# A graph layer on one core: the first product of an edge group in 16-bit passes over 30 nodes a tile, its sums in shifted windows

## The chip, the cores and the metric

The kernel runs on one core of one Trainium2 chip. Its time is the device time of one execution in microseconds (us), given as the median of several runs. A profile is one execution of its own, with its own time. TensorE is called PE in the profile, its weight loads PEld, VectorE DVE, ScalarE ACT, GpSimd POOL, SyncE SP; a small q (SPq) is the engine's queue of instructions and transfers.

## What is computed

One layer of a graph network: 6250 nodes with 128 features, 100000 edges that are sorted by their destination, four attributes an edge.

```python
src = edge_index[0]
dst = edge_index[1]
msg_in = jnp.concatenate([node_features[src], node_features[dst], edge_features], axis=1)
h = jax.nn.silu(msg_in @ mW1 + mb1)
messages = h @ mW2 + mb2
aggregated = jax.ops.segment_sum(messages, dst, num_segments=N)
upd_in = jnp.concatenate([node_features, aggregated], axis=1)
u = jax.nn.silu(upd_in @ uW1 + ub1)
updated = u @ uW2 + ub2
return layer_norm(node_features + updated, ln_g, ln_b)
```

The result of this is added to the input, and one more normalisation over the features follows. With 16 edges a node on average, and destinations in order, 128 edges in a row cover about 8 nodes, and 1024 about 64.

## The kernel before

**Tables.** The first product is taken apart: a node's part as a source, `x @ mW1[:128]`, goes into a table `tab_a` in DRAM, its part as a destination with the bias, `x @ mW1[128:256] + mb1`, into `tab_b`, and the attributes, transposed, into `ea_d`. `tables()` makes all of `tab_a` and the first two batches (of 512 nodes) of `tab_b` before the edges; `make_b` (L457) makes the other 11 batches during the loop.

**Groups.** Edges are worked on in 98 groups of 1024, that is 8 tiles of 128 edges. In 82 of them (`listed`), POOL gathers the rows of `tab_a` by an indirect transfer for each tile (L234), and each further group goes through the following:

- `load` (L578): SP fetches the group's destinations, spread over 80 partitions (`near`, L435), the 80 rows of `tab_b` that start at the group's first node (`mv`, L584), and its 4 rows of attributes, into rows 80 to 83 of `st` (L585).
- `matrices` (L589): DVE makes two one-hot matrices. `st` has a row for each of the 80 nodes and a column for each edge; the same instruction sums its rows into a column of degrees (`deg_at`, L297). `oh` has a row for each edge and 80 columns a tile.
- `before_rows` (L618): for each tile PE multiplies `st` with `mv` into a PSUM tile `pre`; this picks each edge's destination row and adds the attributes' part. All is in 32 bits. `pre` has two buffers (`wide()`, L164).
- `hidden` (L634): DVE adds the gathered rows (L645), ACT applies silu (L646) to give `h`.
- `sums` (L648): for each tile PE multiplies `h` with `oh`, 112 columns of which 80 are used, and adds up the 8 tiles in one PSUM tile `pt`, of which there is one. Every fourth group a transpose puts the columns of degrees into the same tile.
- `add` and `count` (L689, L679): DVE adds `pt` into the sums `acc` of the batch at the group's place, and the degrees into `deg`; the degrees of four groups at once.

**Sorted groups.** The other 16 groups (`by_sort`) are not gathered: their edges are sorted by source at the start, and PE picks the source rows by 16-bit products with one-hot matrices `O` (`po`), from `tab_a` split into three 16-bit parts. Their products stand between those of the listed groups.

**Order.** Each engine's order is written out by hand: the loop over `listed` (L1179) is a row of stages. Stage j of group g asks for the gathers of the group four ahead and the loads three ahead, makes the matrices two ahead, does the first product one ahead, then the work on sorted groups, then the sums of g, and last (`node_stage`, L790) a part of the work on nodes. Half of the gathers are held until PE has reached a certain product (L1244 to L1258); the place is found from the products' work, counted by `matmul(..., share=)` (L147).

**A guard.** `check_1` to `check_4` test that every destination lies within its group's 80 rows. If not, a slow general path (L1360) does all edges again.

Of the kernel before, what the change touches and what calls it, by code (L numbers as in the profile page):

```python
# [10 lines left out]
F32 = mybir.dt.float32  # L11
# [16 lines left out]
def kernel(  # L28
# [28 lines left out]
    W = 80  # L57
    WS = 112
    NW = NP + W
    AW = 768  # L60
    K1 = W + ED
# [146 lines left out]
    w_row_i = first.tile([P, W], I32, name="w_row_i")  # L208
    nc.gpsimd.iota(w_row_i, pattern=[[1, W]], base=0, channel_multiplier=0)
# [13 lines left out]
    tab_b = dram.tile([NW, H], F32, name="tab_b")  # L223
    sd = dram.tile([4, QN * GE], F16, name="sd")
    ea_d = dram.tile([ED, NG * GE], F32, name="ea_d")
# [3 lines left out]
    def fetch(g):  # L229
# [20 lines left out]
        ceil_i, pattern=[[BN * P, NB + 1], [0, G]], base=BN * P - W, channel_multiplier=0  # L250
    )
    pos_i = first.tile([R, P], I32, name="pos_i")
# [9 lines left out]
    if rest:  # L262
        nc.vector.memset(dst_l[low:NG], N)
    nc.sync.dma_start(dst_l[:low], dst[: low * GE].rearrange("(p j) -> p j", j=GE))
# [8 lines left out]
    dst_l = dst_l[:NG]  # L273
    w_row = ps1.tile([P, W], F32, name="w_row")
# [17 lines left out]
    deg_s = []  # L292
    for k in range(3):
        deg_s.append(consts.tile([W, P], F32, name=f"deg_s{k}"))
        nc.vector.memset(deg_s[k], 0.0)

    def deg_at(g):  # L297
        s, i = divmod(g - 1, 4) if g else (-1, 0)
        return deg_s[(s + 1) % 3], 32 * i

    def deg_col(g):
        t, c = deg_at(g)
        return t[:, c : c + 1]
# [19 lines left out]
    def lists_1():  # L323
        base_c = first.tile([NG, 1], F32, name="base_c")
        nc.vector.tensor_copy(base_c, dst_l[:, 0:1])
        rel_n = first.tile([P, GE], F32, name="rel_n")[:NG]
        nc.vector.tensor_scalar(rel_n, dst_l, base_c, None, op0=OP.subtract)
        parts.update(base_c=base_c, rel_n=rel_n)
        nc.vector.memset(floor_i[:, 0:1], 0)
        nc.vector.memset(floor_i[:, last[NB - 2] + 1 :], batches[NB - 1][0] * P)  # L330
        nc.vector.memset(ceil_i[:, 84 + G // 2 :], batches[NB - 1][0] * P - W)
        nc.vector.memset(ceil_i[:, 92 + G // 2 :], NP)
        for g in range(NG):
            k = made_for(g)
            usual = (g + G // 2) // G
            if k < usual and g >= G:
                nc.vector.memset(
                    ceil_i[:, g + G // 2 : g + G // 2 + 1],
                    sum(n for _, n in batches[: k + 1]) * P - W,
                )  # L340

    def lists_2():
# [12 lines left out]
        nc.vector.tensor_copy(base_f, to_row(parts["base_c"], NG))  # L355
        parts["base_f"] = base_f

    def lists_3():
# [3 lines left out]
        nc.vector.tensor_scalar(base_p, p_b[:, :NG], p_col, None, op0=OP.add)  # L362
# [6 lines left out]
        nc.vector.tensor_tensor(base_i, base_f, lim, op=OP.min)  # L369
# [12 lines left out]
    mid = (W - 1) / 2  # L382

    def check_1():
        parts["far"] = first.tile([NG, 2], F32, name="far")
        nc.vector.tensor_reduce(parts["far"][:, 0:1], parts["rel_n"], AX.X, OP.max)

    def check_2():
        far = parts["far"]
        nc.vector.tensor_reduce(far[:, 1:2], parts["rel_n"], AX.X, OP.min)  # L390
# [33 lines left out]
    def attribute_rows(c):  # L424
        t = turn.tile([EQ, ED, EJ], F32, name="ea_t")
        nc.scalar.copy(t, ea_l.pop(c).rearrange("q (j d) -> q d j", d=ED))
        to = ea_d[:, c * EC : (c + 1) * EC]
        nc.scalar.dma_start(to.rearrange("d (q j) -> q d j", q=EQ), t)

    def destinations(g):  # L430
        near[g] = work.tile([P, GE], I32, name="near")[:W]
        n = min(GE, E - g * GE)
        if n < GE:
            nc.vector.memset(near[g][:, n:], N)
        nc.sync.dma_start(  # L435
            near[g][:, :n],
            dst[g * GE : g * GE + n].rearrange("(o e) -> o e", o=1).to_broadcast([W, n]),
        )
# [18 lines left out]
    def make_b(k):  # L457
        i0, n = batches[k]
        pm = bank()
        product(k, 1, pm)  # L460
# [1059 lines left out]
```

## Time and profile before

| | |
|---|---|
| Median of 3 runs | 1079.45 us (1077.62 to 1081.79) |
| Profiled execution, device time | 1078.25 us |
| its span, first to last instruction | 1076.5 us |
| mean granted clock of TensorE | 0.863 |
| instructions | 17905 |
| bytes moved by DMA | 108.94 MB, 101 GB/s |
| gathers, POOL L234 | 654 of about 0.95 us, 0.30 us between two |
| first gather from tab_a | at 68.6 us |
| last gather | issued at 1045.2 us |

The page of a profile gives busy time by engine, then the chain of work that ended last: from the last instruction back to what released it, and so on to the start, with shares of the span. It then lists groups of like instructions, as `line engine op out<-in shapes xcount | busy us, mean ns of one | idle time before them and what ended it`. Most products are recorded on the helper's lines, L148 (`matmul`) and L151 (`transpose`), so they are told apart by what they write: `pre`, `pt`, `po` and `pn`. Matmuls are pipelined, so the mean duration of one is longer than the time from one to the next.

### The profile page before, as it was taken

The page shows a single profiled execution, that of the slowest core. Times are in us where ns is not written, and L with a number is a line of the kernel's source. Part 1 is how long each engine was busy: PE and PEld are TensorE (multiplying, and loading weights), DVE is VectorE, ACT ScalarE, POOL GpSimd, SP SyncE. Part 2 cuts the span into 40 slices and gives each one's busy share as a digit, 9 for nine tenths or more (in the row PEclk, how much of TensorE's full clock was granted, in tenths as well). Part 3 has the DMA queues.
Part 4 walks back from the last instruction along what each step waited for, and adds up shares of the span by engine and source line. Part 5 has one row for each costly group of instructions (what it writes and reads, how often), then busy time and mean ns, then how long its engine had stood idle before and what let it go on. Part 6 is the DMA issues. An engine that isn't in the chain of part 4 may idle for free.

```text
span 1076.5 us, 17905 instructions
## 1 busy us (share of the span) xinstructions
PE 807.8 (75%) x6479; PEld 687.8 (64%) x6479; DVE 558.1 (52%) x1357; ACT 404.1 (38%) x543; POOL 641.9 (60%) x665
## 2 busy tenths in 40 slices
PE   5548557668878788877877878777878877877874
PEld 4548455566757576666776666666577666676653
DVE  3463677843555283555373555444374445473282
ACT  1122114533343354344344353343253344363142
POOL 6646557765656666565666566556566566666550
PEclk8778779789888989798998989879879788999795
DMA  9544315342424252525163443424343434242220
GB/s 231 140 114 117 93 57 143 87 101 81 114 85 116 72 137 76 121 75 131 57 152 84 117 109 97 110 80 100 87 112 93 99 92 120 71 111 81 85 77 25
DMA packets 86890, 108.94 MB, mean 101 GB/s; under 512 B 22348, under 2 KB 63456, under 8 KB 86794
## 3 DMA queue, kind: packets, MB, share of 16 engines
q1 hardware_dynamic: 52498, 58.26, 21.3%
q0 software_dynamic: 20928, 42.90, 15.2%
q10 hardware_dynamic: 13368, 6.56, 2.3%
q8 instruction: 53, 0.87, 0.4%
q14 instruction: 43, 0.35, 0.1%
HBM read 96.26 MB, written 11.40 MB: 100 GB/s over the span
## 4 chain that ended last, share of the span: by engine, by line
PE 52%; issue 16%; DVE 13%; another core or an unknown queue 7%; ACT 5%; DMA 3%; POOL 2%; SPq 1%; DVEq 0%; ACTq 0%; POOLq 0%
PE pt L148 14%; PE po L148 14%; PE pre L148 13%; PE pn L148 8%; PE pn L151 2%; POOL ga L234 2%; DMA ga<-tab_a,src_i 1%; DVE st L593 1%; DVE oh L603 1%; ACT h L646 1%; DVE ga L645 1%; ACT O L1027 1%; PE pre L151 1%; DVE O L1023 1%
## 5 line engine op out<-in xcount | busy, mean ns | idle before, releaser
L234 POOL DMA_INDIRECT ga<-tab_a,src_i x614 | 601.9, 980 | 380.4 <-issue 202.4
L148 PE MATMUL pre<-mv,st 128*128 128x128 f32 x1308 | 202.3, 310 | 27.4 <-issue 12.8
L148 PEld LDWEIGHTS pre<-mv,st 128*128 128x128 f32 x1308 | 190.5, 225 | 40.3 <-issue 29.2
L148 PE MATMUL pt<-oh,h 128*128 128x112 f32 x1308 | 191.5, 305 | 25.6 <-issue 12.6
L148 PEld LDWEIGHTS pt<-oh,h 128*128 128x128 f32 x1308 | 180.1, 218 | 39.5 <-issue 24.3
L646 ACT ACTIVATE h<-ga 128x1024 f32<-128x1024 f32 (+1 forms) x78 | 81.1, 1042 | 317.7 <-DVE ga L645 222.6
L692 DVE TENSOR_TENSOR acc<-acc,pt 128x80 f32 x98 | 23.3, 238 | 341.3 <-PE pt L148 104.1
L148 PE MATMUL po<-O,A_low 128*128 128x157 bf16 (+47 forms) x896 | 163.8, 225 | 22.3 <-issue 22.3
L148 PE MATMUL po<-O,A 128*128 128x156 bf16 (+37 forms) x1376 | 140.2, 227 | 36.6 <-issue 33.0
L148 PEld LDWEIGHTS <-A 128*128 128x128 bf16 x1376 | 112.4, 104 | 58.3 <-issue 57.3
L645 DVE TENSOR_TENSOR ga<-ga,pre 128x1024 f32<-128x1024 f32 (+1 forms) x78 | 93.3, 1197 | 54.7 <-PE po L148 22.0
L593 DVE TENSOR_SCALAR_CACHE_REDUCE st<-near,base_p 80x1024 f32<-80x1024 int32 x82 | 103.4, 1261 | 11.9 <-issue 10.4
L148 PEld LDWEIGHTS <-A_low 128*128 128x128 bf16 x896 | 91.0, 103 | 20.6 <-issue 20.3
L1027 ACT ACTIVATE O<-sc,p_less 128x512 bf16<-128x512 f16 x128 | 84.8, 711 | 1.4 <-DMA sc<-sd 1.4
L1028 ACT ACTIVATE O<-O,ones 128x1024 bf16<-128x1024 bf16 x64 | 73.5, 1148 | 2.1
L603 DVE TENSOR_TENSOR oh<-w_row,rel 128x640 f32<-128x640 f32 x82 | 66.9, 816 | 0.8
L151 PE MATMUL pn<-ident,hT 128*128 128x128 f32 x128 | 23.2, 310 | 45.1 <-issue 10.2
L1070 ACT ACTIVATE hT<-po 128x512 f32<-128x512 f32 x32 | 19.0, 593 | 91.4 <-PE po L148 51.7
L234 POOL DMA_INDIRECT ga<-in_x_dram,src_i x40 | 38.3, 959 | 23.2 <-issue 9.9
L151 PEld LDWEIGHTS pn<-ident,hT 128*128 128x128 f32 x128 | 15.5, 154 | 51.1 <-issue 24.3
L148 PE MATMUL pt<-oh,h_s 128*128 128x112 f32 x256 | 34.8, 290 | 12.6 <-ACT h_s L1079 7.9
L148 PE MATMUL pn<-Oc,at_s 128*128 128x512 f32 x64 | 37.8, 675 | 8.0 <-issue 5.6
(221 smaller groups left out, 921.9 us busy)
## 6 DMA issues: line engine op xcount, KB each, us to landing
near<-in_dst_dram SPq DMA_DIRECT2D x81, 320.0 KB
ga<-tab_a,src_i POOLq DMA_INDIRECT x614
sc<-sd SPq DMA_DIRECT2D x16, 512.0 KB
mv<-tab_b SPq DMA_DIRECT2D x82, 40.0 KB
tab_a<-A SPq DMA_DIRECT2D x11, 256.0 KB
tab_b<-o SPq DMA_DIRECT2D x11, 256.0 KB
out_dram<-o ACTq DMA_DIRECT2D x11, 256.0 KB
x<-in_x_dram SPq DMA_DIRECT2D x10, 256.0 KB
```

The lines of the kernel that those rows point to most:

```text
L148: counted(nc.tensor.matmul(to, *operands, **flags), to, share)
L151: counted(nc.tensor.transpose(to, *operands), to)
L234: ins = nc.gpsimd.indirect_dma_start(out=rows[g][:, i, :], out_offset=None, in_=x if g < RAW else tab_a[:, :], in_offset=bass.IndirectOffs ...
L593: nc.vector.tensor_scalar(stbuf[turn_of(g) % NST][:W], near.pop(g), base_p[:W, g : g + 1], 0.0, op0=OP.is_equal, op1=OP.add, accum_out=deg ...
L603: nc.vector.tensor_tensor(oh[g][:, :n, :W], w_row[:, None, :].to_broadcast([P, n, W]), rel[:, g, :n, None].to_broadcast([P, n, W]), op=OP. ...
L645: nc.vector.tensor_add(s[:, i], s[:, i], p[:, i])
L646: nc.scalar.activation(h[:, i], s[:, i], AF.Silu)
L692: nc.vector.tensor_add(to, to, pt[:, :W])
L1023: nc.vector.tensor_scalar(O[:, j], key, p_rows[:, r : r + 1], None, op0=OP.is_equal)
L1027: nc.scalar.activation(O[:, j], key, AF.Square, bias=p_less[:, r : r + 1])
L1028: nc.scalar.activation(O[:, 2:], O[:, 2:], AF.Relu, bias=ones[:, 0:1], scale=-1.0)
L1070: nc.scalar.activation(now["hT", half], now.pop("po"), AF.Silu)
```

## The change

The group's nodes get a grid: the first node is rounded to a multiple of 8, and tile i looks only at 30 nodes that start 8 i nodes after the group's first.

- **First product.** `st` has 90 rows, 30 nodes in three 16-bit parts each, and 36 rows of attributes (three parts of the attributes times three of their weights); `mv` has 8 blocks of columns, one for each tile. Each tile takes one 16-bit product with 126 rows. The one-hot `st` is made from 16-bit offsets (`off_d`), compared with the row number divided by three.
- **Tables.** `tab_b` stays for the sorted groups; beside it stands `tab_p`, the same in three 16-bit parts, in the order that lets one row of `mv` be 2 KB in a row. A load takes four transfers for `mv`.
- **Sums.** `oh` is filled in 32 of 112 columns, the other 80 stay zero. Tile i adds its 112 columns at column 8 i of `pt`, so `pt` is cleared first by a product of zeros over 256 columns. Degrees come from four products of a column of ones with `oh`, into the same tile. The sums are 88 columns wide.
- **Splitting.** Making a batch of `tab_p`, or a chunk of attributes, is a chain of steps (`begin`, `high`, `middle`, `low`) that are taken at four places in a stage; their PSUM tile is one of the two of `pre`.
- **Weights.** The work of the 16-bit products, of the clearing and of the degrees counts a quarter in the gathers' pacing.

```diff
+    S = 8
+    V, VS, VW = 30, 32, 112
+    WP = S * (G - 1) + VW
+    W = S * (G - 1) + VS
+    D = W // S
+    KB, K1 = 3 * V, 3 * V + 9 * ED
...
+    def b_steps(k, pm):
...
+        def begin():
+            for i in range(BN):
+                matmul(
+                    pm[:m, i, :], xT[k][:, i : n * P : BN], w1[:, 1, :], start=True, stop=True
+                )
+
+        def high():
+            nc.vector.tensor_add(v, v, b1[:m, None, :].to_broadcast([m, BN, H]))
+            nc.scalar.copy(t[:, :, 0], v)
+            tb = node.tile([P, BN, H], F32, name="o")[:m]
+            nc.scalar.copy(tb, v)
...
+        def middle():
+            nc.vector.tensor_sub(v, v, t[:, :, 0])
+            nc.scalar.copy(t[:, :, 1], v)
+
+        def low():
+            nc.vector.tensor_sub(t[:, :, 2], v, t[:, :, 1])
+            d0 = (i0 * P + F) // S
+            for u in range(S // BN):
+                nc.sync.dma_start(
...
-        nc.sync.dma_start(mv[turn_of(g) % NM][:W], tab_b[bass.ds(bases[g], W), :])
-        nc.sync.dma_start(stbuf[turn_of(g) % NST][W:K1], ea_d[:, g * GE : (g + 1) * GE])
+        to = mv[turn_of(g) % NM].rearrange("r i f -> r (i f)")
+        for a in range(D - G + 1):
+            n = min(S, V - a * S)
+            nc.sync.dma_start(
+                to[3 * S * a : 3 * S * a + 3 * n],
+                tab_p[:n, :, bass.ds(bases[g] + a, G), :].rearrange("b s d f -> (b s) (d f)"),
+            )
+        cols = slice(g * GE, (g + 1) * GE)
+        nc.sync.dma_start(
+            stbuf[turn_of(g) % NST][KB:K1],
+            ea_d[:, cols].rearrange("(o r) e -> o r e", o=1).to_broadcast([3, 3 * ED, GE]),
+        )
...
         nc.vector.tensor_scalar(
-            stbuf[turn_of(g) % NST][:W],
-            near.pop(g),
-            base_p[:W, g : g + 1],
-            0.0,
-            op0=OP.is_equal,
-            op1=OP.add,
-            accum_out=deg_col(g),
+            stbuf[turn_of(g) % NST][:KB], near.pop(g), third[:KB], None, op0=OP.is_equal
         )
         oh[g] = ohbuf[turn_of(g) % NST]
         nc.vector.tensor_tensor(
-            oh[g][:, :n, :W],
-            w_row[:, None, :].to_broadcast([P, n, W]),
-            rel[:, g, :n, None].to_broadcast([P, n, W]),
+            oh[g][:, :, :VS],
+            w_row[:, : G * VS].rearrange("p (i w) -> p i w", w=VS),
+            rel[:, g, :, None].to_broadcast([P, G, VS]),
...
             matmul(
-                pre[g][:, i, :], st[:, i, :], mv[turn_of(g) % NM], start=True, stop=not raw
+                pre[g][:, i, :], st[:K1, i, :], mv[turn_of(g) % NM][:K1, i, :],
+                start=True, stop=not raw, share=1 / 4,
             )
...
+    def cleared(pt):
+        matmul(pt, none[:, : pt.shape[0]], none, start=True, stop=False, share=1 / 4)
+
+    def degrees(g, pt):
+        to = pt[0:1, WP : WP + W]
+        if g in by_sort:
+            transpose(to, deg_s[by_sort[g] % 2], ident[:W, :W])
+            return to
+        for a in range(D - G + 1):
+            matmul(
+                to[:, a * S : (a + G) * S], ones[:, 0:1], oh[g][:, :, a * S : (a + 1) * S],
+                start=False, stop=g == NG - 1 and a == D - G, share=1 / 4,
+            )
+        return to
...
+            cleared(pt)
+            if g < NG - 1:
+                degrees(g, pt)
+            for i in range(n):
+                matmul(
+                    pt[:, i * S : i * S + VW], h[:, i, :], oh[g][:, i, :],
+                    start=False, stop=i == n - 1,
+                )
...
+        chain = []
+        for k in range(2, NB):
+            if j == x_stage(k) + 2:
+                chain = b_steps(k, wide()[:, :BN])
...
+                chain = [None] + attribute_steps(c, wide().rearrange("p i f -> p (i f)"))
...
+        go_on()
         sorted_ahead(j)
...
         matrices(ahead(g, 2))
+        go_on()
...
         hidden(ahead(g, 1))
+        go_on()
...
         add(g, sums(g))
+        go_on()
```

`attribute_steps` is built like `b_steps`: `high` copies a chunk's attributes on ACT, `middle` and `low` subtract on DVE and copy on ACT. At the start, `fill_we` splits the attributes' weights and writes them to DRAM, `fill_mv` loads them into the rows 90 to 125 of each `mv`, and `fill_ends` writes the zeros around `tab_p`. The guard tests the offsets within a tile, 0 to 29.

## What I expected of it

> **What bounds the kernel now.** I read the page's busy shares first, then the chain that ended last, then the same chain in order of time, which has the price of one pass.
>
> ```profile
> PE 807.8 (75%) x6479; PEld 687.8 (64%) x6479; DVE 558.1 (52%) x1357; ACT 404.1 (38%) x543; POOL 641.9 (60%) x665
> ...
> PE 52%; issue 16%; DVE 13%; another core or an unknown queue 7%; ACT 5%; DMA 3%; POOL 2%; SPq 1%; DVEq 0%; ACTq 0%; POOLq 0%
> PE pt L148 14%; PE po L148 14%; PE pre L148 13%; PE pn L148 8%; PE pn L151 2%; POOL ga L234 2%; DMA ga<-tab_a,src_i 1%; DVE st L593 1%; DVE oh L603 1%; ACT h L646 1%; DVE ga L645 1%; ACT O L1027 1%; PE pre L151 1%; DVE O L1023 1%
> ```
>
> TensorE is the bound, but not all the time: half of the chain is its products, and 16% is time in which nothing shown holds it. The change works on two terms of the last line, `pre` (first product) and `pt` (sums), and on two small ones, `st` and `oh`. The rows of these four:
>
> ```profile
> L148 PE MATMUL pre<-mv,st 128*128 128x128 f32 x1308 | 202.3, 310 | 27.4 <-issue 12.8
> ...
> L148 PE MATMUL pt<-oh,h 128*128 128x112 f32 x1308 | 191.5, 305 | 25.6 <-issue 12.6
> ...
> L593 DVE TENSOR_SCALAR_CACHE_REDUCE st<-near,base_p 80x1024 f32<-80x1024 int32 x82 | 103.4, 1261 | 11.9 <-issue 10.4
> ...
> L603 DVE TENSOR_TENSOR oh<-w_row,rel 128x640 f32<-128x640 f32 x82 | 66.9, 816 | 0.8
> ```
>
> 1308 records for 654 tiles: a 32-bit product is two passes. The 310 ns are the modelled end of a pipelined matmul, not the spacing. The spacing is in the chain in order of time, where a run of products stands with its length (start, length, what):
>
> ```profile
> 498.91 3.21 PE pre L148 x16
> ...
> 512.53 1.78 PE pre L148 x16
> 514.32 3.77 PE po L148 x60
> ```
>
> Sixteen passes (eight tiles) take 1.78 us where the clock is full, 0.111 us a pass, and 3.21 us, 0.20 a pass, where it is halved. Sixty products in 16 bits, each with weights of its own, take 3.77 us, 0.063 apiece.
>
> **The first product.** A tile's two 32-bit passes (0.222 us) become one 16-bit pass of 128 columns. Nearest row, in the timeline of TensorE (start, length, group):
>
> ```profile
> 515.57 0.22 PE L148 MATMUL po<-O,A_low 128*128 128x131 bf16 x1
> 515.63 0.28 PE L148 MATMUL po<-O,A_high 128*128 128x135 bf16 x2
> ```
>
> The next product starts 0.06 us after one of 131 columns, so I take 0.06: 73% of `pre`'s time goes. On the engine: the mean clock 0.863 means 27% of the time at half rate, so a tile saves 0.73 x 0.162 + 0.27 x 0.28 = 0.194 us, and 654 tiles 127 us. On the chain: `pre` L148 is 13% of 1076.5, 140 us; 1308 of its 1486 passes are these (the others multiply by w1), 123 us; 73% of that is 90. The difference lies beside other waits. I take **-90**, ends -90 and -127.
>
> **The sums and degrees.** The eight tile products keep 112 columns and two passes, so nothing changes there. Added per listed group (82): one 16-bit product of zeros over 256 columns (`cleared`; 0.12 us, twice the 128-column price) and four 32-bit degree products of 64 columns with one weight column, eight passes. No row is like these. Nearest: `po<-st_s,mv_s`, 32 bits, whose two passes of 512 columns take 1.02 us together at 0.594 each, so the second starts 0.43 after the first, 0.84 ns a column: 0.054 for 64, 0.056 with a little for each start. Lower end 0.028 (16-bit products of 14 to 51 columns stand about that far apart), upper end 0.111, a pass at full weights. At 0.056: 8 x 0.056 + 0.12 = 0.57 us, times 1.16 for the clock (1/0.863), times 82: 54 us on the engine (33 to 96). `pt` is on the chain for 14%, 151 us, of 1564 passes x 0.135 = 211, 71%: **+39** (23 to 68). Gone are 26 transposes of the degree columns, 0.13 us each on the chain: **-3**. The deg additions on DVE stay one per group (97 at 230 ns before); they no longer come four in a burst, but each now holds `pt`, of which there is one, 0.24 us longer; neither gains.
>
> **The one-hot matrices.** `st` (1.261 us and an accumulator read of 0.078) loses its sum and is 16 bits both sides. Nearest: `O<-sc,p_rows`, two of 512 columns in 0.62 us, so 0.62 for 1024. `oh` shrinks from 640 to 256 columns, 0.816 to about 0.42 by its slope. DVE is relieved of about 1.1 us a group, 92 us, but the chain has the two at 1% each, 21 us: half goes, **-11**.
>
> **Node products and attributes as chains of steps.** Each of 11 batches in the loop adds two DVE passes over 512 PSUM columns (0.69 us, as L462) and two more ACT copies (0.59); each of 9 attribute chunks two DVE passes and two ACT copies of 500. DVE gets 27 us, ACT 24 us, on engines with half their time free: +3 on the path. More matters where they sit: a chain takes one of the two `pre` buffers for a whole stage (`wide()`), in 20 stages. In that stage `before_rows` for g+1 has to wait for the addition that empties g's buffer, and in the next for the chain's `low` step, which DVE does after acc and deg: 0.24 + 0.24 + 0.6 us behind the sums. Without the chains TensorE would go straight on. Queued behind the waiting product are the picked products, sums and everything after. Lower end 0, since sums(g) needs the same addition a little later; upper end in the rivals. The batch's product itself moves from the end of a stage to its start, right behind the copy of xT that ACT makes after its picks; in the trace TensorE met that copy 3 times for 8.7 us in all. I take 0.5 us a stage for all of this, **+10**.
>
> **Loads.** SP issues six transfers a group instead of three (near; four of mv; st), each 0.31 to 0.38 us with its register move: 1.2 us more of SP per stage of 12 us. SP also gets two tab_p stores a batch, which wait for `low` and stand ahead of the next loads; in the trace SP stood 134 us behind the old tab_b store without holding anyone. The loads are asked for a stage or more ahead, so I cost this at 0; without that cover it is the 1.2 us per group. A rule speaks against it: the Trainium skill (DMA: Bandwidth & Descriptors, "Why a DMA increments its semaphore by 16 and not by 1") says a transfer is spread over the largest number of engines, at most 16, that divides the outer dimension of both sides. For near that is 15, for three of mv 12, for the attributes ([3, 12] rows) only 3. By the trace, 100 GB/s at 39% of 16 engines is 16 GB/s per busy engine: 72 KB on three is 1.5 us, on sixteen 0.3. No row shows such a transfer, but 1.2 us within a stage of lead costs nothing; against the rule alone, 82 x 1.2 = 98 us, I take the lead.
>
> **The start.** Before the first gather from tab_a (68.6 us) SP gets some 25 more transfers, DVE the splitting of the weights (it waits for a load issued at about 17 us, where DVE before went on at 13.7), and two b chains and one attribute chain run to their end at once, where DVE waits for ACT and ACT for DVE, about 3 us each. DVE and TensorE have idle pieces of 2 to 5 us there, which take about half: **+10**, 4 to 20.
>
> **Sum.** 1076.5 - 90 + 39 - 3 - 11 + 3 + 10 + 10 = 1034.5, plus 1.75 around the span (1078.25 - 1076.5): **1036**. The three runs' median is 1.2 above the profiled one, so 4% under it.
>
> **Rivals.** *All of TensorE's saving counts* (127, with 33 to 54 given back): the same sum is 992 to 1014, middle 1003. For: 634 of the 800 us below are TensorE's. Against: 16% "issue" and idle pieces that end with ACT and DVE.
>
> *The clock takes it back.* Stretch, TensorE busy and count, PEld, DVE, ACT, POOL, clock:
>
> ```profile
> 25.00:50.00 25.00, 15.14 (x82) 13.80 (x82) 11.38 (x22) 3.32 (x5) 16.30 (x18) 0.70 0.47 131
> ...
> 125.00:150.00 25.00, 11.98 (x73) 10.75 (x73) 18.37 (x59) 3.37 (x6) 14.39 (x16) 0.70 0.26 73
> ...
> 200.00:1000.00 800.00, 633.92 (x5445) 538.52 (x5446) 405.15 (x912) 331.83 (x448) 488.19 (x504) 0.89 0.39 100
> ```
>
> Where TensorE is busy 79% it is granted 0.89, where 48 to 61%, 0.70. The Trainium skill (TensorE: Matmul & The Clock Gate, "Why this matters for your kernels") asks for no idle gap over about 3 us, or the rate is halved; taking work out between waits lengthens gaps. By the row I keep the clock: the busy share falls by a few points at most, since the stages shorten too. By the rule: of the 634 us 58 go (0.8 of 127 - 54), and 576 x (0.89/c - 1) come on top; 27 at a clock of 0.85, so 1063, and 42 at 0.83, so no change. A slower clock also makes TensorE busier, so I do not expect it.
>
> *Slower: the borrowed `pre` buffer.* If in the 20 chain stages TensorE really stops until g's gathers are in and DVE has got through its queue, the price is that of a late gather, in the list of waits (waiter, awaited: total, times, longest):
>
> ```profile
> ACT h L646 <- DMA ga<-tab_a,src_i: 47.1, 12, 11.7
> ```
>
> 3.9 us on average. 20 x 4 = 80 in place of 10: 1106. It decides from (42 + 10)/20 = 2.6 us a stage on. Against: that wait was met in only 12 of 78 stages.
>
> *The gathers* are no bound: 614 x 1.25 us (0.95 and 0.30 of issue) after 79 us and a tail of 30 give 877; they are released by products, whose weights (a quarter for the 16-bit ones) follow the new prices, so their lead stays. *The guard:* offsets outside 0 to 29 would send everything to the general path; with the reference's dst they are 4 to 24, so no.
>
> **Numbers.** Forecast 1036 (1008 to 1064): 0.50. All counts, 1003: 0.12. Clock, 1050 to 1085: 0.13, of it 0.04 faster, 0.07 same, 0.02 slower. Slower, 1106: 0.25. Faster 0.66, same 0.07, slower 0.27; 0.5%, 5.4 us, is about what can be told from no change. The range reaches down to 985 and up to 1105, leaving 0.05 below and half of the slower case above.
>
> **What would show it.** `pre<-mv,st` as 654 records spaced 0.06 us; degree passes near 0.056; `st` near 0.6 us and `oh` near 0.42; clock still 0.85 or more; first gather from tab_a near 79 us; in chain stages no wait of TensorE for DVE over a us. It is wrong if degree passes cost 0.11, if the clock in the middle is under 0.83, or if `pre` waits for `ga` or `low` for some us in 20 places.

## The result, and the profile after

The changed kernel takes **1122.59 us** (median of 4 runs, 1119.83 to 1124.37); the kernel before, run beside it, 1080.62 (1077.62 to 1083.15). The ratio is **1.0387**, with a 95% interval of 1.0351 to 1.0423: 42 us slower, where 1036 us was forecast. The profiled execution took 1119.83 us, its span is 1118.1 us.

In three of the five sets of runs below, both kernels were some 17% quicker than in the profiled pair (the kernel before 892 to 896 us; in the two others 1075 to 1078 us), so each run is compared with the kernel before of its own set, as a ratio, and the two conditions are called *long* and *short*. In both, the change loses about the same: 1.039 and 1.036.

The page after: busy shares, then the chain that ended last, by engine and by line.

```profile
PE 819.2 (73%) x6559; PEld 651.0 (58%) x6559; DVE 482.0 (43%) x1330; ACT 433.3 (39%) x602; POOL 660.9 (59%) x667
...
PE 53%; issue 14%; DVE 10%; ACT 6%; another core or an unknown queue 6%; DMA 1%; POOL 1%; DVEq 1%; SPq 0%; ACTq 0%; POOLq 0%
PE pt L154 21%; PE po L154 15%; PE pn L154 8%; PE pre L154 6%; PE pn L157 2%; ACT O L1148 1%; DVE ga L743 1%; DVE O L1144 1%; ACT O L1149 1%; DMA ga<-tab_a,src_i 1%; DVE deg L805 1%; POOL ga L241 1%; DVE st_s L1126 1%; DVE y L850 1%
```

TensorE's share of the chain is what it was. Within it the first product (`pre`) went from 13 to 6%, as was meant, and the sums with clearing and degrees (`pt`) from 14 to 21%. The products themselves became cheaper, as forecast (group rows after, and a run of eight first products from the chain in order of time):

```profile
L154 PE MATMUL pre<-mv,st 126*128 126x128 bf16 x654 | 68.4, 247 | 21.5 <-DMA mv<-tab_p 6.9
...
L154 PE MATMUL pt<-oh,ones 128*1 128x64 f32 x648 | 62.7, 244 | 11.7 <-issue 11.1
...
L696 DVE TENSOR_SCALAR st<-near,third 90x1024 bf16<-90x1024 f16 x82 | 39.6, 483 | 17.4 <-issue 17.4
...
L700 DVE TENSOR_TENSOR oh<-w_row,rel 128x256 f32<-128x256 f32 x82 | 33.7, 411 | 0.5
...
492.87 0.45 PE pre L154 x8
```

Eight first products in 0.45 us are 0.056 us each, and one degree product follows another at the same distance (0.056 us, the median of the trace). The busy time of the first product fell from 202.3 to 68.4 us, the degree products take 62.7, `st` 0.48 us instead of 1.26, `oh` 0.41 instead of 0.82. The stretch from 200 to 1000 us (TensorE, weight loads, DVE, ACT, POOL, then the granted clock) says what became of it:

```profile
200.00:1000.00 800.00, 616.46 (x5232) 484.84 (x5232) 337.51 (x866) 341.63 (x473) 489.57 (x484) 0.83 0.42 107
```

Before, 633.92 us of these 800 were TensorE's, at a clock of 0.89. It now stands idle for more of them, and what it does it does at 0.83.

**A ledger by gathers.** The 614 gathers from `tab_a` run one after the other on POOL and end 25 to 30 us before the span does, so the time splits into: when the first begins, how long they are busy, how long POOL idles between them, and a tail. The rows, of before and then of after (count, busy us, mean ns, idle us before them):

```profile
L234 POOL DMA_INDIRECT ga<-tab_a,src_i x614 | 601.9, 980 | 380.4 <-issue 202.4
```

```profile
L241 POOL DMA_INDIRECT ga<-tab_a,src_i x614 | 620.7, 1011 | 394.3 <-issue 219.1
```

The first begins at 68.60 us before, at 82.69 after (in the timeline of POOL: start, length):

```profile
82.69 1.12 POOL L241 DMA_INDIRECT ga<-tab_a,src_i  x1 [4.95 <-DMA tab_a<-A]
```

So: 14.1 us from a later start, 18.8 from longer gathers, 13.9 from more idle time between them; together 46.8, and the tail is 5 us shorter. The ledger tells where time stands, not what caused it; the experiments were made for that.

### The profile page after: what moved, and what is told of

The parts are those of the page before. It is cut to its first block, busy times and chain, and to the rows that moved or that the text cites. A ratio compares the mean times of both kernels' runs of the same rounds, so it can differ in the third digit from the quotient of the medians.

```text
span 1118.1 us, 19033 instructions
## 1 busy us (share of the span) xinstructions
PE 819.2 (73%) x6559; PEld 651.0 (58%) x6559; DVE 482.0 (43%) x1330; ACT 433.3 (39%) x602; POOL 660.9 (59%) x667
## 2 busy tenths in 40 slices
DMA packets 115306, 120.44 MB, mean 108 GB/s; under 512 B 50535, under 2 KB 79103, under 8 KB 115203
## 4 chain that ended last, share of the span: by engine, by line
PE 53%; issue 14%; DVE 10%; ACT 6%; another core or an unknown queue 6%; DMA 1%; POOL 1%; DVEq 1%; SPq 0%; ACTq 0%; POOLq 0%
PE pt L154 21%; PE po L154 15%; PE pn L154 8%; PE pre L154 6%; PE pn L157 2%; ACT O L1148 1%; DVE ga L743 1%; DVE O L1144 1%; ACT O L1149 1%; DMA ga<-tab_a,src_i 1%; DVE deg L805 1%; POOL ga L241 1%; DVE st_s L1126 1%; DVE y L850 1%
## 5 line engine op out<-in xcount | busy, mean ns | idle before, releaser
L241 POOL DMA_INDIRECT ga<-tab_a,src_i x614 | 620.7, 1011 | 394.3 <-issue 219.1
L154 PE MATMUL pt<-oh,h 128*128 128x112 f32 x1308 | 206.0, 318 | 13.3 <-issue 12.9
L810 DVE TENSOR_TENSOR acc<-acc,pt 128x88 f32 x98 | 23.9, 244 | 426.1 <-PE pt L154 134.7
L154 PEld LDWEIGHTS pt<-oh,h 128*128 128x128 f32 x1308 | 188.2, 227 | 28.7 <-issue 22.0
L154 PE MATMUL po<-O,A_low 128*128 128x157 bf16 (+47 forms) x896 | 170.1, 231 | 14.5 <-issue 14.4
L154 PE MATMUL po<-O,A 128*128 128x156 bf16 (+37 forms) x1376 | 145.9, 234 | 40.5 <-issue 21.9
L154 PEld LDWEIGHTS <-A 128*128 128x128 bf16 x1376 | 117.9, 108 | 60.9 <-issue 60.3
L154 PEld LDWEIGHTS <-A_low 128*128 128x128 bf16 x896 | 94.2, 106 | 13.8 <-issue 13.7
L154 PE MATMUL pre<-mv,st 126*128 126x128 bf16 x654 | 68.4, 247 | 21.5 <-DMA mv<-tab_p 6.9
L154 PEld LDWEIGHTS <-st 126*128 126x128 bf16 x654 | 54.7, 114 | 32.6 <-issue 26.5
L154 PE MATMUL pt<-oh,ones 128*1 128x64 f32 x648 | 62.7, 244 | 11.7 <-issue 11.1
L154 PE MATMUL pt<-oh_s,h_s 128*128 128x88 f32 x256 | 48.0, 358 | 27.0 <-ACT h_s L1200 13.7
L154 PEld LDWEIGHTS pt<-oh_s,h_s 128*128 128x128 f32 x256 | 45.0, 268 | 28.4 <-ACT h_s L1200 14.1
L154 PEld LDWEIGHTS pt<-oh,ones 128*1 128x1 f32 x648 | 41.3, 92 | 31.9 <-issue 25.3
L154 PE MATMUL pre<-w,xT 128*128 128x128 f32 (+2 forms) x186 | 42.3, 392 | 24.0 <-ACT xT L486 13.3
L154 PEld LDWEIGHTS pre<-w,xT 128*128 128x128 f32 (+2 forms) x186 | 38.2, 292 | 27.5 <-ACT xT L486 14.9
```

Of the source, the lines that this page charges most:

```text
L154: counted(nc.tensor.matmul(to, *operands, **flags), to, share)
L241: ins = nc.gpsimd.indirect_dma_start(out=rows[g][:, i, :], out_offset=None, in_=x if g < RAW else tab_a[:, :], in_offset=bass.IndirectOffs ...
L810: nc.vector.tensor_add(to, to, pt[:, :W])
```

## The experiments

**What the first product is worth alone, and TensorE's slack** (set 1, short; before 892.04 us). *e1_first16*: the kernel before with its first product alone in 16 bits.

```diff
-        mv.append(consts.tile([P, H], F32, name=f"mv{k}"))
+        mv.append(consts.tile([P, H], BF16, name=f"mv{k}"))
...
-        stbuf.append(consts.tile([P, GE], F32, name=f"st{k}"))
+        stbuf.append(consts.tile([P, GE], BF16, name=f"st{k}"))
...
-        nc.sync.dma_start(mv[turn_of(g) % NM][:W], tab_b[bass.ds(bases[g], W), :])
+        nc.sync.dma_start(mv[turn_of(g) % NM][:W], tab_16[bass.ds(bases[g], W), :])
```

> The kernel before, with the first product alone in one 16-bit pass a tile (its operands are rounded to one 16-bit part, so node and attribute terms lose digits; one small copy and one transfer a batch are added to make the 16-bit table). Nothing else of the change is in it: 80 columns, degrees by sum and transpose, no chains of steps. The forecast's step (-90 us for the first product, clock kept at 0.89 between 200 and 1000 us): 985 to 1000 us. The theory that the freed TensorE time turns into waits and the clock falls with it: clock 0.82 to 0.85 in that stretch and 1045 to 1075 us.

Measured: 879.14 us, ratio 0.985 (0.979 to 0.991), that is 13 us. Its stretch from 200 to 850 us, then the row of its gathers:

```profile
200.00:850.00 650.00, 514.83 (x4849) 427.58 (x4848) 402.82 (x915) 330.37 (x454) 491.77 (x512) 0.88 0.50 120
...
L235 POOL DMA_INDIRECT ga<-tab_a,src_i x614 | 600.2, 978 | 189.6 <-issue 151.2
```

The clock is 0.88, where the kernel before has 0.92 in the same stretch (e5, shown with e12 below). So the clock fell here too, but it is not what set the time. 189.6 us of idle time over 614 gathers is 0.309 us each, the time POOL takes between two when nothing holds it: the gathers follow each other without a stop, from 65.6 to 855 us. They are the floor of this run, and no product that gets cheaper moves it. (This run's start is 9.6 us later than that of e5 below, so its middle gained some 23 us.)

*e2_nodeg* and *e3_twice* (same set) take the degree products out of the changed kernel and issue its first product twice.

```diff
-        for a in range(D - G + 1):
+        for a in range(D - G + 1) if g == NG - 1 else ():
             matmul(
                 to[:, a * S : (a + G) * S], ones[:, 0:1], oh[g][:, :, a * S : (a + 1) * S],
```

> The changed kernel without the four degree products of each listed group (the clearing and the addition of the degree row stay, so degrees of those groups are zero). If the degree products stand on the path: 648 passes less at 0.055 us (full clock) to 0.107 us (half), so 35 to 55 us less, 1068 to 1088 us. If waits and the clock set the time: less than 15 us gained, over 1107 us, with a lower clock than 0.83 between 200 and 1000 us.

```diff
+            for r in range(1 if raw else 2):
                 matmul(
                     pre[g][:, i, :], st[:K1, i, :], mv[turn_of(g) % NM][:K1, i, :],
```

> The changed kernel with each tile's first product issued twice (the second overwrites the first with the same values; groups 0 to 4 once). If TensorE's products are the path: 614 passes more at 0.056 to 0.107 us, 35 to 60 us more, 1157 to 1183 us. If idle time and the clock it brings set the time: within 15 us of 1122, and the clock between 200 and 1000 us back up from 0.83 by 0.02 or more.

Without degrees 917.51 us (ratio 1.029, 1.022 to 1.036), with the product doubled 935.82 (1.050, 1.044 to 1.057), where the changed kernel has 1.036 in the next set: 6 us less and 13 us more, for some 35 to 60 us of work taken out or put in. The sets differ and their intervals reach 6 to 9 us to either side, so the 6 us cannot be told from nothing. *e4_ownbank* gave the chains of steps a PSUM bank of their own:

```diff
-    w_row = ps1.tile([P, G * VS + W], F32, name="w_row")
+    w_row = consts.tile([P, G * VS + W], F32, name="w_row")
...
-                chain = b_steps(k, wide()[:, :BN])
+                chain = b_steps(k, chain_bank())
```

> The changed kernel with the chains of steps in a PSUM bank of their own (the row of column numbers, w_row, moves from PSUM to SBUF to make room, and the bias row ub2 is held once instead of four times). The rival of the borrowed pre buffer: 20 stages x 2 to 4 us come back, 1040 to 1085 us. If the borrowed buffer costs no more than the 0.5 us a stage of the forecast: 1108 to 1122 us.

928.24 us, ratio 1.041 (1.035 to 1.047): nothing came back. The edit is not clean, since `oh` now reads `w_row` from SBUF, and the mean gather rose to 1036 ns, from 1010 and 1013 in the two runs beside it.

**The pair on one chip, and two edits of the changed kernel** (set 2, short; before 895.51 us). *e5_before* and *e6_after* are the two kernels unchanged; e5 is a single run, of 901.27 us.

> The kernel before, unchanged, so that its trace stands beside those of the other runs of the same chip. If the gathers are the bound where the kernel takes about 890 us: 614 gathers of tab_a stand 0.31 us apart nearly throughout and the last ends some 25 us before the span does. If TensorE is the bound: gaps of over 1 us before one gather in ten or more.

> The changed kernel, unchanged, on the same chip as the runs beside it. If its loss comes from the gathers, the ratio to the kernel before stays near 1.04 although the time of both is shorter here: +15 us from a later first gather and 614 x 0.03 us = 19 us from longer ones, 34 us of 892. If it comes from TensorE's clock: the ratio goes with the difference of the clocks, and is under 1.02 where the clock of this kernel is over 0.87.

The changed kernel took 924.18 us, ratio 1.036 (1.026 to 1.045), with a clock of 0.882: the loss is not in proportion to the clock. The rows of the gathers and the first of them in the timeline, before and then after:

```profile
55.97 0.95 POOL L234 DMA_INDIRECT ga<-tab_a,src_i  x1 [0.30 <-issue]
...
L234 POOL DMA_INDIRECT ga<-tab_a,src_i x614 | 600.9, 979 | 215.6 <-issue 156.4
```

```profile
81.20 1.11 POOL L241 DMA_INDIRECT ga<-tab_a,src_i  x1 [4.96 <-DMA tab_a<-A]
...
L241 POOL DMA_INDIRECT ga<-tab_a,src_i x614 | 626.7, 1021 | 192.8 <-issue 143.9
```

Busy and idle together are 816.5 us before and 819.5 after. The cheaper products did take away what idle time there was (0.35 to 0.31 us a gather, so that the changed kernel stands on the gathers' floor as e1 does), and the gathers themselves became longer by as much. What is left is the start: the first gather from `tab_a` begins at 56.0 us before and at 81.2 after.

*Why a gather gets longer*: one that took 2.45 us, in the changed kernel's timeline of POOL and DVE (e6).

```profile
427.31 2.45 POOL L241 DMA_INDIRECT ga<-tab_a,src_i  x1 [0.30 <-DMA ga<-tab_a,src_i]
...
427.98 0.74 DVE L1135 TENSOR_SCALAR Oc<-sc,p_rows 128x1024 f32<-128x1024 f16 x1
428.64 0.60 DVE L1144 TENSOR_SCALAR O<-sc,p_rows 128x512 bf16<-128x512 f16 x2
429.17 0.47 DVE L696 TENSOR_SCALAR st<-near,third 90x1024 bf16<-90x1024 f16 x1
429.56 0.40 DVE L700 TENSOR_TENSOR oh<-w_row,rel 128x256 f32<-128x256 f32 x1
```

An ordinary gather takes 0.94 us. This one ends at 429.76, 0.12 us after `st` does, which closes a row of quick instructions from SBUF to SBUF; `oh`, which reads PSUM, no longer holds it. The Trainium skill (SBUF — State Buffer, "SBUF: two separate sides") says that DVE's quick modes lock GpSimd out of a pair of ports that both share, for the whole instruction, so that it can't write the descriptors of its transfers. The trace agrees with it, and not at this gather alone: 67 gathers of e6 took over 1.1 us, 28 of e5, and for 33 of the 67 the last DVE instruction to end before they do is `st` or `oh`. e4, where `oh` lost its PSUM operand, fits too. Before, `st` was summed by the same instruction, took 1.26 us, and none of the 28 ends behind it. A rival for a part of it, more and smaller packets (115306 in all, 86890 before), was not varied alone. Two edits were to show what longer gathers and a later start cost. *e7_slowst* goes back to the summing form:

```diff
-            stbuf[turn_of(g) % NST][:KB], near.pop(g), third[:KB], None, op0=OP.is_equal
+            stbuf[turn_of(g) % NST][:KB], near.pop(g), third[:KB], 0.0,
+            op0=OP.is_equal, op1=OP.add, accum_out=unused[:KB],
```

> The changed kernel with the one-hot st made by the form of instruction that also sums its rows, as before (the sum is not used; about 1.26 us instead of 0.48). If the quick 16-bit form holds up POOL: the mean gather goes back from 1011 ns to 990 or less, and the time falls by 10 to 20 us where gathers are the bound, although DVE has 64 us more to do. If DVE's own time counts: the time rises by 10 us or more. If neither: within 5 us.

The gathers shortened, to 997 ns, and the time rose. Its four runs, 937.61 to 954.09 us, lie too far apart for a ratio, but all above e6's 920.06 to 930.96: DVE's 64 us more of work cost more than the shorter gathers gave. The price of the locked ports could not be read this way. *e8_start* relieved the start a little (its other half, not shown, has POOL make `w_row_i` ahead of the gathers):

```diff
-    fills = [fill_we] + [lambda t=t: fill_mv(t) for t in mv] + [fill_ends]
-    fills += [lambda t=t: nc.vector.memset(t[:, :, VS:], 0.0) for t in ohbuf]
+    fills = [lambda t=t: nc.vector.memset(t[:, :, VS:], 0.0) for t in ohbuf]
+    fills += [fill_ends, fill_we] + [lambda t=t: fill_mv(t) for t in mv]
```

> The changed kernel with the start relieved: POOL makes the row of column numbers (w_row_i) before the first gathers instead of behind the first eight, and the splitting of the attribute weights (fill_we) is asked for after the clearing of oh instead of first. The first gather from tab_a comes at 72 to 77 us instead of 80 to 83. If the start is passed on to the end: the time falls by as much. If the middle takes it up: under 3 us.

A miss: the first gather moved to 79.8 us only, and the time was 925.86, ratio 1.034 (1.025 to 1.042). `w_row` no longer waited (after, DVE stands until 16.0 us for POOL's numbers, which come behind eight gathers), but DVE then stood as long for the attribute weights, whose load had moved back as well.

**The two causes apart and together** (set 3, short; before 894.10 us). *e9_swap* exchanges `oh` and `st` within `matrices`, which adds nothing. *e10_start2* loads the weights at once, splits them five batches later and takes the starting chains one step a batch:

```diff
-            if k == 6:
-                for step in attribute_steps(0, selected()):
-                    step()
+            if k in (7, 10):
+                chain = b_steps((k - 7) // 3, bank())
+                chain.pop(0)()
...
+            if k >= 7:
+                chain.pop(0)()
+                if more:
+                    more.pop(0)()
```

> The changed kernel with the two one-hot instructions of a group in the other order: oh (which reads w_row from PSUM) before st. Nothing is added. If POOL is held up while DVE runs quick 16-bit instructions one behind the other (two O, then st), oh between them lets it in: the mean gather falls from 1.01 to 1.02 us to under 1.00, and the time by 8 to 18 us. If the longer gathers come from the transfers (more and smaller packets): mean and time as before the edit, within 4 us.

> The changed kernel with its start reordered: the row of column numbers is made by POOL ahead of the first gathers, the attribute weights are loaded at once but split only five batches later, and the starting chains of steps (two of tab_b, one of attributes) are taken one step a batch instead of each to its end. The first gather from tab_a comes at 62 to 72 us instead of 80 to 83. If the gathers are the bound from there on, the time falls by as much as that moves, 10 to 18 us; if the middle has another bound, by less than 5.

> The changed kernel with both edits, oh before st and the reordered start. If the two are all of the loss: 20 to 32 us less than the changed kernel, a ratio to the kernel before of 0.995 to 1.015. If they are not the cause: 1.03 or more.

e9: 924.11 us (1.031, 1.025 to 1.038). e10: 910.49 (1.019, 1.013 to 1.026). e11: 911.59 (1.018, 1.009 to 1.026). Most of the start is passed on: the first gather is at 82.1 us in e9, at 65.8 in e10 and at 64.8 in e11, and the times are 13.6 and 12.5 us below that of e9, about three quarters of the 16.3 and 17.3 us. The order of `oh` and `st` is all that parts e11 from e10. It brought gathers of 1003 ns instead of 1013, as the locked ports would have it, and not a microsecond (e10, then e11):

```profile
L248 POOL DMA_INDIRECT ga<-tab_a,src_i x614 | 621.9, 1013 | 202.5 <-issue 144.8 <-DMA ga<-tab_a,src_i 14.6 <-DMA tab_a<-A 9.8
```

```profile
L248 POOL DMA_INDIRECT ga<-tab_a,src_i x614 | 616.0, 1003 | 216.3 <-issue 153.5 <-PE pt L154 13.7 <-DMA ga<-tab_a,src_i 9.8
```

Idle time between gathers grew by more than the gathers shrank: with POOL eased, it waits for products again (13.7 us for `pt`). It looks as if two limits lay close together; no run here moves the second alone.

*e12_before_twice* (same set) doubled the disputed term in the kernel before:

```diff
+            for r in range(1 if raw else 2):
                 matmul(
-                    pre[g][:, i, :], st[:, i, :], mv[turn_of(g) % NM], start=True, stop=not raw
+                    pre[g][:, i, :], st[:, i, :], mv[turn_of(g) % NM],
+                    start=True, stop=not raw, share=1 / (1 if raw else 2),
                 )
```

> The kernel before with each tile's first product issued twice (same values; groups 0 to 4 once), 614 x 2 passes more at 0.111 us or 0.20 us: TensorE gets 136 us more at full clock. By the forecast's step, in which a pass of the first product counts by its share of the chain: 90 to 140 us more. If the gathers are the bound and TensorE has slack: less than half of that, under 65 us.

953.42 us, ratio 1.068 (1.061 to 1.075): 59 us for 136 us of products (at full clock). And the clock rose; from 200 to 850 us, the kernel before (e5) and then this one:

```profile
200.00:850.00 650.00, 561.89 (x5240) 484.46 (x5238) 384.59 (x870) 312.86 (x426) 472.38 (x491) 0.92 0.50 119
```

```profile
200.00:850.00 650.00, 601.25 (x5792) 535.50 (x5790) 367.90 (x827) 296.82 (x404) 435.36 (x455) 0.97 0.47 112
```

Work added is paid for by less than half, work removed (e1, 127 us of it by the forecast's count) by a fifth at most: the kernel before stood just above the floor (e5: 215.6 us of idle time, where e1 has 189.6).

**The long condition** (set 4; before 1077.54 us), in which the result itself was measured and the gathers are no floor: POOL idles 0.6 us between two on average, 0.30 as a rule and over 1 us at 121 places. *e13_first16_start* is e1 with the attribute weights loaded at once, and it is the experiment that tests the forecast's main term where it was made.

> The kernel before with the first product alone in 16 bits (one rounded part, as in the first experiment), and its attribute weights loaded at once but converted four batches later, so that the start is that of the kernel before. If the gathers are the floor: first gather from tab_a at 55 to 60 us, 614 gathers 1.285 us apart, a tail of 25: 870 to 880 us, ratio 0.97 to 0.985. If the first product had been worth its share of the chain: ratio under 0.93.

1073.91 us against 1077.54, ratio 0.9964 (0.9939 to 0.9989): **3.6 us**. Its first gather begins at 71.9 us, 3.3 later than before, so with the old start it would be some 7 us. Its stretch from 200 to 1000 us:

```profile
200.00:1000.00 800.00, 575.27 (x4966) 470.96 (x4964) 402.52 (x912) 334.79 (x456) 486.82 (x506) 0.84 0.40 98
```

TensorE's 633.92 us at a clock of 0.89 are 564 at full clock; 575.27 at 0.84 are 483. At the old clock the 483 would take 543. So 91 us of work did go, the size of the forecast's term; 32 of it came back as slower clock, 59 became idle time. And the gathers, which are released by products, went on at the pace that they had:

```profile
L235 POOL DMA_INDIRECT ga<-tab_a,src_i x614 | 600.5, 978 | 380.0 <-issue 218.4
```

600.5 + 380.0 us here, 601.9 + 380.4 before. Where the chain went instead is on its page:

```profile
PE 36%; DVE 17%; issue 17%; another core or an unknown queue 12%; ACT 5%; DMA 3%; SPq 2%; POOL 1%; DVEq 1%; ACTq 0%; POOLq 0%
PE pt L148 12%; PE po L148 11%; PE pn L148 7%; PE pre L148 4%; DVE ga L665 2%; DVE st L612 2%; PE pn L151 2%; DVE oh L622 2%; POOL ga L235 1%; DVE O L1043 1%; DVE st_s L1025 1%; DVE deg L706 1%; DVE bn L725 1%; ACT h L666 1%
```

TensorE's share fell from 52 to 36%, that of `pre` from 13 to 4%, and the span stayed. DVE (13 to 17%), unknown releasers (7 to 12%) and small shares of others took the place.

*e14_first16_quick* adds the quick `st` (16-bit offsets, no sum).

> The run beside it with st made by the quick 16-bit comparison of 16-bit offsets instead of the form that sums its rows (the degrees of the listed groups stay zero; DVE has 64 us less to do). If the quick form itself holds up POOL: mean gather 1.00 us or more instead of 0.978, and with gathers one behind the other a time 10 to 20 us longer than the run beside it. If the longer gathers have another origin: mean 0.98, time equal or shorter.

1062.26 us, ratio 0.989 (0.983 to 0.994), 12 us less than e13. The row of its gathers:

```profile
L236 POOL DMA_INDIRECT ga<-tab_a,src_i x614 | 599.7, 977 | 367.1 <-issue 212.5
```

They begin at 68.5 us, 3.4 earlier than in e13, which is a part of the 12; DVE's relief and the smaller loads of `near` are not told apart in the rest. Here the quick form did not lengthen the gathers. So the quick form alone is not the cause of the longer gathers; what else in the changed kernel is, stays open.

*e15_both_nodeg* is e11 without degree products, *e16_both_pt2* e11 with two halves of a bank for `pt` in turn:

```diff
-        return ps1.tile([P, 2 * P], F32, name="pt")
+        if not pts:
+            pts.append(ps1.tile([P, 2, 2 * P], F32, name="pt"))
+        half[0] = 1 - half[0]
+        return pts[0][:, half[0]]
```

> The changed kernel with the reordered start and oh before st, and without the four degree products of a listed group (degrees of those groups are zero). If the degree products are the second limit that took the shorter gathers' place in the experiment with both edits: gaps between gathers back from 0.338 to 0.31 us, 15 to 20 us less than that run's 911.6, ratio 0.995 to 1.005. If not: over 905 us.

> The changed kernel with the reordered start and oh before st, and with two halves of the PSUM bank taken in turn for pt, so that the clearing and the degrees of the next group need not wait until DVE has added up this one. If that wait is the second limit: gaps between gathers back to 0.31 us, 12 to 20 us less than 911.6 us. If not: within 5 us.

1108.49 us (1.024, 1.015 to 1.033) and 1114.33 us (1.034, 1.027 to 1.040). Both were expected in absolute times of the short condition, so only the ratios can be judged, and both missed. Between them lie 6 us, as in e2; but the two differ in `pt` as well and their intervals overlap, so this is not shown to be the price of the degree products. The second half of `pt` brought nothing that shows: e16 stands 0.5% below the changed kernel's 1.0387, and its first gather, at 78.1 instead of 82.7 us, is 0.4% of that.

**The chains of steps** (set 5, long; before 1074.85 us). *e17_endchain* takes each chain whole, in the bank of `pn`; *e18_onepart* also leaves out its middle and low steps, and so rounds to one part.

```diff
+            if j == x_stage(k) + 2:
+                for step in b_steps(k, bank()):
+                    step()
...
-        for k in range(2, NB):
-            if j == x_stage(k) + 2:
-                chain = b_steps(k, wide()[:, :BN])
...
-                assert not chain
-                chain = [None] + attribute_steps(c, wide().rearrange("p i f -> p (i f)"))
+                for step in attribute_steps(c, bank().rearrange("p i f -> p (i f)")):
+                    step()
```

> The changed kernel with its chains of steps in the loop put where the kernel before made its tables: the 11 node batches whole at the end of a stage, behind the turned x, in the bank pn; the 9 attribute chunks whole at the start of a stage, in pn too. No pre buffer is borrowed and begin no longer stands at the start of a stage; the arithmetic and the transfers are the same. If the place and the borrowed buffer are what the middle loses by: ratio to the kernel before 1.01 to 1.025 instead of 1.036 to 1.039. If the arithmetic and its hand-overs between DVE and ACT are: 1.03 to 1.06. If neither: as the changed kernel.

> The run beside it with, in the loop, only the highest of the three 16-bit parts made (the other two are zero, so that node and attribute terms are rounded to one part; the transfers are the same): no middle and low steps, that is 40 DVE passes of 0.68 us and 20 ACT copies of 0.57 us less, and no going back and forth. If the chains are all that the middle loses: ratio 1.00 to 1.02. If the loss is elsewhere (loads, clearing, degrees): over 1.03.

e17: 1148.02 us, 1.065 (1.061 to 1.069). e18: 1117.84 us, 1.041 (1.037 to 1.044), no better than the changed kernel. Taken whole, a chain makes TensorE wait for DVE (waits of TensorE in e17: total, times, longest):

```profile
PE pn L157 <- DVE ea_t L466: 30.1, 4, 10.1
```

The steps spread over a stage avoid that. e18 has neither the splitting nor the borrowed buffer, and is no quicker for it. It does not quite clear them: its own whole chains make TensorE wait 10.2 us for ACT (3 waits for `o`, L523), and as much could be hidden by that.

**No version here that computes all that the change computes is quicker than the kernel before.** The best with all three 16-bit parts is e10, 910.49 us beside 894.10. e1, e13 and e14 are quicker, but round the node terms to one part, and e14 leaves degrees out.

## Why the prediction was wrong, point by point

- **The step that failed: "On the chain: `pre` L148 is 13% of 1076.5 ... 73% of that is 90".** The prices were right (0.056 us a tile where 0.06 was taken), and 91 us of TensorE's work went. The step took a share of the chain of waits for time that would be saved. Alone, in place of 90 us, the saving was worth 3.6 us in the long condition and 13 (23 without its own later start) in the short one. The chain names what the time was spent on, along one path; in e13 it ran over other work in the same time, and what was taken from TensorE came back as waiting (59 us) and as a slower clock (32). Half of the chain was not TensorE's (16% "issue", 13% DVE, 7% unknown), and I had quoted that.
- **The sum without this step comes out at the measured time, by luck.** With 3.6 us in place of 90 the forecast would be 1122, and 1122.59 was measured. But the largest of the terms that are left, +39 for degrees and clearing, is not what the runs show.
- **The rival "the clock takes it back" was right as to the clock, 0.83, and it was not the whole.** I kept 0.89 because shorter stages would keep TensorE as busy; the stages did not shorten. Of the 91 us in e13, the clock took 32. The rule that I set aside, that idle gaps cost the clock, was the better guide. In the short condition the clock between 200 and 850 us is 0.92 before and 0.93 after (0.90 and 0.88 over the whole run), and the loss was the same: the clock is one of the ways by which the saving goes, not its cause.
- **"*The gathers* are no bound: ... 877".** e1 ran at 879 us: in the short condition this is the floor. That the two agree so closely is partly luck, since the sum took 1.25 us a gather and a start at 79, and e1 has 1.29 and 65.6. In the long condition the gathers are no floor; there they are held, it seems by a loop of products, DVE, ACT and gathers, of which I can't name the slowest part: removing work from TensorE (e13), degree products (e15), the wait for `pt` (e16) or the chains (e18) moved it by about 1% or less each, the earlier start of e15 and e16 taken off.
- **Degrees and clearing, +39.** The degree passes cost 0.056 us, as taken. On the page `pt` rose from 14 to 21% of the chain, some 84 us; taking the degree products out moved the end by 6 us, which is within the noise: the same mistake with the other sign. Clearing was not tried alone.
- **The start, +10 (4 to 20).** It is +14 in the profiled pair and +25 in the short condition, where about three quarters of what is taken off it reach the end (e10, e11). I counted transfers and chains at half their time, and missed that `w_row_i` had moved behind the first eight gathers on POOL's queue. This is the one part of the loss that is shown and, in part, mended.
- **The borrowed `pre` buffer, the forecast's slower rival, 1106.** The sign came true and the mechanism did not. In the trace after, the products into `pre` (L154) wait 6.3 us for DVE in five places and 13.3 us for `xT` of ACT in five, not 4 us in each of 20; and undoing it in e4 and in e18, neither of them a clean edit, gained nothing. Of the signs of being wrong that I had named, this one and dear degree passes did not come, and the clock, at 0.83, stood on its limit.
- **Gathers, "their lead stays".** I did not ask whether a quicker instruction on DVE holds up POOL. The gathers became longer by 31 ns (42 in the short condition), 19 to 26 us over 614; exchanging two instructions took 10 ns off (e11 against e10) without moving the end, so this is not shown to be a loss of its own.

What is settled: of the 90 us forecast for the first product, 3.6 came in the long condition and 13 in the short one, and the later start is a part of the loss. By the ledger it is 14 of the 42 us in the long condition, though that it is passed on was shown in the short one. The other 28 us are open. They lie in the middle (by the ledger 32.7 us over 98 groups, 0.33 a group), and taking out the chains, the degrees or the wait for `pt` gave back 10 us at most (e15, in which the exchanged order counts too). The four loads a group for `mv`, the clearing, the longer gathers and the weights by which products release gathers were not varied singly.

## What to carry to other kernels

Read a share of the chain of waits as the most that removing it can bring, and expect less: here 13% of the chain was worth 0.4 to 1.5%. Before a term is taken off, double it: here that moved the end by less than half of the work added (e12), and taking the work away moved it by a fifth at most. And write a ledger for the resource that runs from start to end (here the gathers: first, busy, idle, tail); it shows at once whether a saving can reach the end. Look also at what a setup instruction stands behind when it is moved: here one was put behind eight gathers, and DVE stood until 16.0 us.

## What was not expected of the hardware

The same program took 1077 us and 895 us in different sets, once on the same chip (sets 1 and 5), with nearly equal durations of the instructions of DVE, ACT and POOL. What differs are waits that nothing in the profile ends, or only an unknown releaser (`remote`). In the kernel before, long condition:

```profile
PE po L148 <- issue: 61.1, 86, 3.1
...
POOL ga L234 <- remote: 50.5, 35, 2.6
```

All waits of the first kind come to 130.7 us of TensorE there; in the short condition (e5) it has two, 8.8 us in all, and no engine waits for `remote`. The clock differs too, 0.863 and 0.903. Why, no run here tells.
